# A selective-scan network: the first 512 tokens' chain written out in order, side work behind the chunk-end copies, eight scan buffers

## Chip, cores and metric

The kernel runs on one core of one Trainium2 chip. The metric is the device time of one execution in microseconds (us). Engines are named as in the profile: PE (TensorE), with its weight loads as PEld, DVE (VectorE), ACT (ScalarE), POOL (GpSimd) and SP (SyncE, which here issues all data transfers).

## What is computed

Two layers on an input of 4 images of 64 x 64 tokens with 128 channels, all in float32. The change touches only the first block, a two-dimensional selective scan (L is 4096 tokens, DI is 256 channels, N is 16 states, K is 4 directions):

```python
xz = layernorm(x) @ in_proj_w.T;  xh, z = split(xz);  z = silu(z)
xc = silu(depthwise_conv3x3(xh) + conv_b)                 # 256 channels, 64 x 64
xs = [xc by rows, xc by columns, both reversed]           # K = 4 orders of the tokens
dts, B, C = split(x_proj_weight @ xs)                     # 8 + 16 + 16 rows
delta = softplus(dt_projs_weight @ dts + bias);  A = -exp(A_logs)
for t in tokens:                                          # for each of 256 channels and 16 states
    h = exp(delta[t] * A) * h + (delta[t] * xs[t]) * B[t]
    y[t] = sum over states of h * C[t]
y = layernorm(sum of the 4 directions + D * xs) * z;  x = x + y @ out_proj_w.T
```

After it come a mixture of experts with token choice, a block of row, column and token projections, and a spectral convolution.

## The kernel before

**The scan.** The 4 batches, 4 directions and 8 pieces of 512 tokens make 128 chunks; each chunk has 16 steps, one for each state. A step works on two halves of 128 channels. ACT makes `da` (the exponential of delta times A, L2026) three steps ahead; SP loads `bc` (B and C of that state, spread over all partitions, L2016) five steps ahead into 6 buffers; DVE makes `db = du * B` in PSUM (L2078) and then runs the recurrence into `hh` (L2084); POOL saves the last column (`hst`, L2096) and multiplies `hh` by C (L2097); PE adds the result into `y` by eight transposing matmuls (L2124). `hh` has HH = 7 buffers, so DVE's scan of a step waits for the transposes of the step seven earlier. These waits are taken one step early, by a dependency set by hand.

**A chunk's sizes.** `step_sizes` (L1894) prepares delta (`dl`) and `dx = delta * xc` of the next chunk while the present one runs, one piece a step: load `dts` and `xc`, project (`dt_ps`), softplus on ACT with a correction on POOL, sum on PE (`dl_ps`), product on POOL. At the last step of a chunk `into_psum` (L2003) copies `dx` with ACT into the two PSUM tiles `du` that DVE reads; they have one buffer, so the copies wait for the last db of the chunk, and the first db of the next chunk waits for them.

**Side work.** Everything else of the first part (normalising, input projection, convolution, row projections and gating of the other batches, experts) is a Python generator that yields an estimated cost with each piece. `deal` (L1960) is called twice a step, pulls pieces until what was made reaches what is due, and hangs what it pulled behind the scan's latest instruction on each engine. What is due grows by `WEIGHT[batch] / (chunks * (16 - len(BUSY)) * 2)` a call; in the steps listed in BUSY nothing is dealt. Side work has two PSUM banks (`bank`, L274), and evictions are put off to the next piece (`evict_soon`). The recording layer then orders each engine's instructions itself, within the dependencies.

**The front.** The first batch can't hide behind a scan. `front` (L404) works in groups of 512 tokens (g = 0 to 7): sums for the norm on DVE (L429, L431), reciprocal root on ACT, refinement on POOL (L435 to L441), normalising on ACT, transposes on PE (L448), input projection (L454), copies into the padded image `xh` (L457), a 3 x 3 convolution, sigmoid on ACT (L398 to L401), gate on POOL (L482), row projections (L489), stores of dts, B and C (`put_bc_of`). For groups 0 and 1 the convolution's half 0 runs on DVE (nine taps, L478 and L480) and half 1 on PE (matmuls with diagonal matrices, L467); groups 2 and 3 are done together, both halves on DVE. All of groups 0 to 3 and the input of group 4 are issued ahead of the scan, as are the sizes of chunk 0 (`prelude`); groups 4 to 7 are dealt beside the scan. At the start of chunks 0 to 7 pieces are pulled until the rows of the next chunk's group have been issued. Then come the columns (the transposed image and its projections), batches 1 and 2, gates and filters.

Of the kernel before, what the change touches and what calls it, by code (L numbers as in the profile page):

```python
# [32 lines left out]

FIRST = 1
WEIGHT = (1180.0, 1008.0, 1346.0, 927.0)

BUSY = (2, 3)
XB = 6
HH = 7
AHEAD = 4  # L40
# [66 lines left out]
def kernel(  # L107
# [58 lines left out]
    early = tc.tile_pool(name="fr_x", bufs=XB, side="right")  # L166
# [7 lines left out]
    for g in range(5):  # L174
        load_x0(g)
# [7 lines left out]
    nc.sync.dma_start(cb, conv_b)  # L183
    xp = wp.tile([P, 2, 2, 104], F32, name="xp")
# [6 lines left out]
    nc.sync.dma_start(aneg, a_logs)  # L191
    dsk = wp.tile([P, K, 2], F32, name="dsk")
# [17 lines left out]
    for h in range(2):  # L210
        for t in range(9):
            nc.vector.tensor_scalar(diag[:, h, t, :], ident, cw[:, h, t : t + 1], None, ALU.mult)
# [191 lines left out]
    def front(prelude):  # L404
# [6 lines left out]
        with tc.tile_pool(name="fr", bufs=2) as fr:  # L411
            pools = ExitStack()
            fps = pools.enter_context(tc.tile_pool(name="fr_ps", bufs=2, space=PSUM))
            xps = pools.enter_context(tc.tile_pool(name="fr_xd", bufs=1, space=PSUM))
            xh = [fr.tile([P, H + 2, W + 2], F32, name=f"xh{h}", bufs=1) for h in range(2)]
            for h in range(2):
                nc.gpsimd.memset(xh[h][:, 0, :], 0.0)
                nc.gpsimd.memset(xh[h][:, H + 1, :], 0.0)
                nc.gpsimd.memset(xh[h][:, 1 : H + 1, 0:1], 0.0)
                nc.gpsimd.memset(xh[h][:, 1 : H + 1, W + 1 : W + 2], 0.0)  # L420
            st, xn, vs, sts = {}, {}, {}, {}

            def sums(g):
                s6 = fr.tile([P, 4, 6], F32, name="s6")
                mv = fr.tile([P, 4, 2], F32, name="mv", bufs=4)
                r = fr.tile([P, 4], F32, name="f_r", bufs=4)
                nm = fr.tile([P, 4], F32, name="f_m", bufs=4)
                for q in range(4):
                    nc.vector.bn_stats(s6[:, q, :], x0[g][:, q, :])  # L429
                for q in range(4):  # L430
                    nc.vector.bn_aggr(mv[:, q, :], s6[:, q, :])  # L431
                nc.scalar.activation(r, mv[:, :, 1], AF.Ln, bias=eps6)
                nc.scalar.activation(r, r, AF.Exp, scale=-0.5)
                a = fr.tile([P, 4], F32, name="f_a")
                nc.gpsimd.tensor_scalar(a, mv[:, :, 1], 1.0, 1e-6, ALU.mult, ALU.add)  # L435
                nc.gpsimd.tensor_mul(a, a, r)
                nc.gpsimd.tensor_mul(a, a, r)
                nc.gpsimd.tensor_scalar(a, a, -0.5, 1.5, ALU.mult, ALU.add)
                nc.gpsimd.tensor_mul(r, r, a)
                nc.gpsimd.tensor_scalar(nm, mv[:, :, 0], -1.0, 0.0, ALU.mult, ALU.add)  # L440
                nc.gpsimd.tensor_mul(nm, nm, r)  # L441
                st[g] = nm, None, r

            def spread(g):
                norm_apply(x0[g], x0[g], st[g], 4)
                ps = bank([P, 4, P], "xt_ps")
# [3 lines left out]
                nc.scalar.copy(xn[g], ps.rearrange("c q p -> c (q p)"))  # L450
                nc.sync.dma_start(xn_d[b][:, 512 * g : 512 * (g + 1)], xn[g])
                for h in range(2):
                    ps = bank([P, 8, W], "in_ps")
                    nc.tensor.matmul(  # L454
                        ps, w_in_t[:, h * P : (h + 1) * P], xn[g], start=True, stop=True
                    )
                    nc.scalar.copy(xh[h][:, 1 + 8 * g : 9 + 8 * g, 1 : W + 1], ps)  # L457

            def windows(h, t, r0, rows):
                dy, dx = divmod(t, 3)  # L460
                return xh[h][:, r0 + dy : r0 + dy + rows, dx : dx + W]

            def convolve(g0, n, h, first):
                ps = fps.tile([P, 8 * n, W], F32, name="fcv_ps", tag="cv")
                for g in range(n):
                    for t in range(first):
                        nc.tensor.matmul(  # L467
                            ps[:, 8 * g : 8 * g + 8],
                            diag[:, h, t, :],
                            windows(h, t, 8 * (g0 + g), 8),  # L470
                            start=(t == 0),
                            stop=(t == first - 1),
                        )
                for t in range(first, 9):
                    wt = cw[:, h, t : t + 1]
                    src = windows(h, t, 8 * g0, 8 * n)
# [4 lines left out]
                v, e = sigmoid_of(fr, ps.rearrange("p r w -> p (r w)"), h)  # L481
                nc.gpsimd.tensor_mul(v, v, e)  # L482
                nc.sync.dma_start(xc_d[b][0, h, :, 512 * g0 : 512 * (g0 + n)], v)
                for g in range(n):
                    vs[g0 + g, h] = v[:, 512 * g : 512 * (g + 1)]

            def project(g, ps):
                for h in range(2):
                    nc.tensor.matmul(ps, xp[:, 0, h, :], vs[g, h], start=(h == 0), stop=(h == 1))  # L489
                sts[g] = fr.tile([104, SC], F32, name="xd_st", bufs=3)  # L490
                evict_soon(lambda: nc.scalar.copy(sts[g], ps))

            def rows_of(g):
                project(g, xps.tile([104, SC], F32, name="fxd_ps"))
                put_bc_of(b, g, sts[g])

            for g in range(5):
                sums(g)
            for g in range(5):
                if g + 5 < 8:  # L500
                    load_x0(g + 5)
                    sums(g + 5)
                spread(g)
                if g in (1, 2):
                    for h in range(2):
                        convolve(g - 1, 1, h, 9 * h)
                if g == 2:
                    rows_of(0)
                    prelude(sts[0])
            for h in range(2):  # L510
                convolve(2, 2, h, 0)
            for g in range(1, 4):
                rows_of(g)
            side["rows"] = AHEAD
# [3 lines left out]
            for g in range(5, 8):  # L518
                norm_apply(x0[g], x0[g], st[g], 4)
                yield 1.5  # L520
                ps = bank([P, 4, P], "xt_ps")
                for q in range(4):
                    nc.tensor.transpose(ps[:, q, :], x0[g][:, q, :], ident)
                xn[g] = fr.tile([P, 512], F32, name="xn")
                evict_soon(lambda ps=ps, g=g: nc.scalar.copy(xn[g], ps.rearrange("c q p -> c (q p)")))
                yield 1.0
                settle()
                yield 0.5
                nc.sync.dma_start(xn_d[b][:, 512 * g : 512 * (g + 1)], xn[g])
                for h in range(2):  # L530
                    ps = bank([P, 8, W], "in_ps")
                    nc.tensor.matmul(
                        ps, w_in_t[:, h * P : (h + 1) * P], xn[g], start=True, stop=True
                    )
                    nc.scalar.copy(xh[h][:, 1 + 8 * g : 9 + 8 * g, 1 : W + 1], ps)
                    yield 1.0

            def rows(g):
                project(g, bank([104, SC], "xd_ps"))

            for g in range(AHEAD, 8):
                for h in range(2):
                    ps = bank([P, 8, W], "cv_ps")
                    for t in range(9):
                        nc.tensor.matmul(
                            ps,
                            diag[:, h, t, :],
                            windows(h, t, 8 * g, 8),
                            start=(t == 0),
                            stop=(t == 8),  # L550
                        )
                        if t % 3 == 2:
                            yield 2.6
                    v, e = sigmoid_of(fr, ps.rearrange("p r w -> p (r w)"), h)
# [16 lines left out]
                rows(g)  # L571
# [1311 lines left out]
    with ExitStack() as c0:  # L1883
        pb = c0.enter_context(tc.tile_pool(name="pb", bufs=2))
        slots(3)


# [6 lines left out]
        def step_sizes(b, k, ci, have=None):  # L1894
# [6 lines left out]
            def pieces():  # L1901
                cs = slice(ci * SC, (ci + 1) * SC)
                dts = have
                if dts is None:
                    dts = pb.tile([R, SC], F32, name="dts", bufs=1)
                    nc.sync.dma_start(dts, dts_d[b][k, :, cs])
# [79 lines left out]
        def prelude(st):  # L1986
            sizes[0] = step_sizes(0, 0, 0, st[0:R, :])
            list(sizes[0][3])

        opening = front(prelude)  # L1990
        next(opening)
        side.pop("pool").close()
        dbs = c0.enter_context(tc.tile_pool(name="pb_db", bufs=1, space=PSUM))
# [246 lines left out]
```

## Time and profile before

| what | us |
|---|---|
| median of 3 runs (lowest, highest) | 9501.18 (9497.8, 9502.11) |
| the profiled execution | 9507.07 |
| its span in the trace | 9505.2 |
| first db of the scan, from the span's start | 83.15 |
| last scan ends | about 7711 |
| busy in the span: DVE, PE, POOL, ACT | 8222.5, 7331.8, 6373.1, 6138.1 |
| mean of one scan (with a start value), one db, one da | 1.258, 0.677, 0.718 |
| mean of one POOL product of hh and C | 2.359 |

Times in the trace count from the span's start. A row of a timeline gives start, duration, engine, line, operation, output and inputs, shapes, how many were merged, and in brackets how long the engine was idle before and what ended that. A row of waits gives who waited for whom, the total, the number of times and the longest. On PE a float32 matmul of a 512-wide tile appears as two MATMUL rows, a transposing one as a single row. The program calls fcv_ps the convolution's PSUM tile, sg_e and sg_v the sigmoid's, fxd_ps the row projection's.

### The profile page before, as it was taken

What the parts mean: (1) busy time and instruction counts of PE and PEld (TensorE: products, weight loads), DVE (VectorE), ACT (ScalarE), POOL (GpSimd) and SP (SyncE); (2) the same over time, 40 slices, a digit from 0 to 9 for tenths busy, and PEclk for the clock granted to TensorE, in tenths of its full rate; (3) what the DMA queues carried; (4) which work ended last, traced back from release to release, by engine and by line L of the source; (5) the groups of instructions that cost most, each with busy time, mean ns of one, the idle gap of its engine ahead of it and who ended that gap; (6) DMA issues with size and microseconds to landing.
All of it is one profiled execution on the core that took longest, in us unless ns stands there. A gap on an engine that the chain in (4) does not pass through costs nothing.

```text
span 9505.2 us, 139568 instructions
## 1 busy us (share of the span) xinstructions
PE 7331.8 (77%) x45462; PEld 4748.2 (50%) x45462; DVE 8222.5 (87%) x9171; ACT 6138.1 (65%) x11727; POOL 6373.1 (67%) x5954
## 2 busy tenths in 40 slices
PE   7687886577677777697778777767777677999997
PEld 3444544355444555454545554544555445555553
DVE  8999999989999999999999999999999951566663
ACT  6676767657755676776855677765676744555552
POOL 6788888869788888887878788978888841000000
PEclk8788787678787877798878787878887876999998
DMA  5656566667566656658757667757656673333336
GB/s 161 228 189 218 191 213 223 206 189 243 174 221 224 207 163 207 192 192 256 230 183 244 195 195 233 242 172 239 226 164 207 211 220 95 91 95 95 95 94 181
DMA packets 914957, 1806.23 MB, mean 190 GB/s; under 512 B 86816, under 2 KB 472640, under 8 KB 910520
## 3 DMA queue, kind: packets, MB, share of 16 engines
q1 hardware_dynamic: 914232, 1797.30, 60.1%
q8 instruction: 365, 5.98, 0.3%
q14 instruction: 360, 2.95, 0.1%
HBM read 1554.75 MB, written 242.22 MB: 189 GB/s over the span
## 4 chain that ended last, share of the span: by engine, by line
POOL 23%; PE 20%; issue 11%; DVE 10%; ACT 7%; DMA 6%; SPq 0%; POOLq 0%; DVEq 0%; ACTq 0%
POOL hh L2097 17%; PE sp_ps L1674 10%; DVE hh L2084 4%; DVE wt L1678 3%; PE y L2124 3%; ACT da L2026 2%; DVE db L2078 2%; DMA bc<-bc_d 1%; POOL hst L2096 1%; PE dl_ps L1940 1%; POOL dx L1943 1%; POOL ex L1934 1%; ACT no_sq L352 1%; DMA yk<-y_d 1%; PE yk_ps L790 1%
## 5 line engine op out<-in xcount | busy, mean ns | idle before, releaser
L2097 POOL TENSOR_TENSOR hh<-hh,bc 128x1024 f32<-128x1024 f32 x2048 | 4830.2, 2359 | 365.8 <-DVE hh L2084 203.2
L2084 DVE TENSOR_TENSOR_SCAN hh<-da,hst,db 128x512 f32<-128x512 f32 x3584 | 4375.6, 1258 | 117.3 <-PE y L2124 54.3
L2124 PE MATMUL y<-ident,hh 128*128 128x128 f32 x16384 | 2654.6, 316 | 1233.2 <-POOL hh L2097 1125.3
L2026 ACT ACTIVATE da<-dl,aneg 128x512 f32<-128x512 f32 x4096 | 2776.0, 718 | 1135.4 <-DVE hh L2084 1124.5
L2124 PEld LDWEIGHTS y<-ident,hh 128*128 128x128 f32 x16384 | 2212.5, 163 | 2147.7 <-POOL hh L2097 1502.3
L2078 DVE TENSOR_TENSOR db<-du,bc 128x512 f32<-128x512 f32 x4096 | 2605.0, 677 | 149.6 <-ACT du L2007 128.3
L2096 POOL COPY hst<-hh 128x2 f32<-128x2 f32 x1792 | 336.6, 188 | 695.6 <-DVE hh L2084 629.1
L1678 DVE COPY wt<-sp_ps 128x1024 f32<-128x1024 f32 x512 | 606.0, 1220 | 176.3 <-PE sp_ps L1674 153.2
L1674 PE MATMUL sp_ps<-vt,taps 32*128 32x256 f32 x8192 | 588.7, 399 | 54.7 <-DVE wt L1678 35.1
L2084 DVE TENSOR_TENSOR_SCAN hh<-da,db 128x512 f32<-128x512 f32 x512 | 594.5, 1199 | 12.3 <-PE y L2124 9.7
L1678 ACT COPY wt<-sp_ps 128x1024 f32<-128x1024 f32 x512 | 516.5, 1015 | 102.3 <-PE sp_ps L1674 82.4
L1674 PEld LDWEIGHTS sp_ps<-vt,taps 32*128 32x128 f32 x8192 | 387.9, 184 | 246.9 <-DVE wt L1678 196.8
L1678 DVE COPY zs<-sp_ps 128x1024 f32<-128x1024 f32 x128 | 156.7, 1224 | 353.1 <-PE sp_ps L1674 350.9
L1674 PE MATMUL sp_ps<-wt,ut 128*32 128x256 f32 x8192 | 448.7, 379 | 1.4 <-DVE wt L1678 1.4
L661 PE MATMUL cv_ps<-xh,diag 128*128 128x512 f32 x864 | 402.1, 601 | 2.8 <-ACT sg_v L399 2.5
L1915 PE MATMUL dt_ps<-dts,dtw 8*128 8x512 f32 x508 | 352.3, 794 | 47.0 <-ACT sg_v L399 21.5
L1940 PE MATMUL dl_ps<-ex,ident 128*128 128x512 f32 x512 | 307.0, 688 | 95.2 <-POOL ex L1934 95.1
L1674 PEld LDWEIGHTS sp_ps<-wt,ut 128*32 128x32 f32 x8192 | 264.8, 110 | 193.8 <-issue 23.5
L1943 POOL TENSOR_TENSOR dx<-dl,xc 128x1024 f32<-128x1024 f32 x128 | 302.5, 2363 | 84.0 <-ACT dl L1941 76.0
L1941 ACT COPY dl<-dl_ps 128x512 f32<-128x512 f32 x256 | 148.0, 578 | 306.4 <-PE dl_ps L1940 305.8
L1934 POOL TENSOR_TENSOR ex<-ex,dx 128x1024 f32<-128x1024 f32 x128 | 302.3, 2362 | 59.3 <-ACT dx L1931 52.0
L1678 ACT COPY zs<-sp_ps 128x1024 f32<-128x1024 f32 x128 | 129.5, 1012 | 320.7 <-DMA zf<-zs 168.8
(331 smaller groups left out, 9260.0 us busy)
## 6 DMA issues: line engine op xcount, KB each, us to landing
bc<-bc_d SPq DMA_DIRECT2D x2048, 512.0 KB
xc<-xc_d SPq DMA_DIRECT2D x128, 512.0 KB
y_d<-ys SPq DMA_DIRECT2D x128, 512.0 KB
w1t<-in_w_dram SPq DMA_DIRECT2D x96, 512.0 KB
w2t<-in_w_dram SPq DMA_DIRECT2D x192, 256.0 KB
yk<-y_d SPq DMA_DIRECT2D x128, 256.0 KB
yk<-y_d SPq DMA_DIRECT2D x256, 128.0 KB
zf<-zs SPq DMA_DIRECT2D x512, 64.0 KB
```

Source lines behind the costliest of these rows:

```text
L661: nc.tensor.matmul(ps, diag[:, h, t, :], xh[:, 8 * g + dy : 8 * g + dy + 8, dx : dx + W], start=(t == 0), stop=(t == 8),)
L1674: tc.keep_in_program_order(nc.tensor.matmul(*args, **kw))
L1678: tc.keep_in_program_order(copy(dst, src))
L1934: nc.gpsimd.tensor_sub(ex, ex, dx)
L1940: nc.tensor.matmul(ps, ident, t[:, h], start=t is dl, stop=t is w)
L1943: nc.gpsimd.tensor_mul(dx, dl, xc)
L2026: i_act = nc.scalar.activation(das[t][:, h, :], sizes[t // N][0][:, h, :], AF.Exp, scale=aneg[:, tk, h, t % N : t % N + 1],)
L2078: nc.vector.tensor_mul(db[h], dus[i][h], bcs[s][:, 0, :])
L2084: i_dve = nc.vector.tensor_tensor_scan(o, d0, d1, init, ALU.mult, ALU.add)
L2096: nc.gpsimd.tensor_copy(hsts[t // N][:, :, t % N], hhs[t][:, :, last])
L2097: i_pool = nc.gpsimd.tensor_mul(hhs[t], hhs[t], bcs.pop(t)[:, 1:2, :].to_broadcast([P, 2, SC]))
L2124: i_pe = nc.tensor.matmul(ys[c][:, q, h, :], hhs[t][:, h, q * P : (q + 1) * P], ident, is_transpose=True, start=(n == 0 and k > 0 and q % ...
```

## The change

1. The front is rewritten along the chain of group 0, its order on PE, ACT, DVE and POOL fixed as it is written. Normalising is split over DVE and ACT, refinement of groups 0 to 2 is on DVE; the diagonal matrices are built by POOL (18 products) instead of DVE; the gates of group 0 are one DVE operation each. Ahead of the scan now stand group 0, the input of groups 1 and 2, the taps of group 1 (half 0 on DVE, half 1 on PE), and the sums of all groups. Chunk 0's sizes are made by `first_sizes`, half by half, with DVE's product written straight into `du`. The weights needed first are loaded ahead of x0's later groups.
2. The rest of groups 1 to 7 is dealt beside the scan, all taps on PE; `WEIGHT[0]` rises from 1180 to 1275. ACT work that is pulled at the start of chunks 0 to 7 is ordered behind the exponentials that were issued two steps before.
3. Step 14 joins BUSY, and after the copies of `into_psum` the anchor for dealt ACT work is the second copy.
4. HH rises from 7 to 8. x0 gets 8 buffers instead of 6, and the pools for `du` and `db` change places.

The core of the diff:

```diff
-WEIGHT = (1180.0, 1008.0, 1346.0, 927.0)
-BUSY = (2, 3)
-XB = 6
-HH = 7
-AHEAD = 4
+WEIGHT = (1275.0, 1008.0, 1346.0, 927.0)
+BUSY = (2, 3, 14)
+HH = 8
...
-    for g in range(5):
+    for g in range(2):
         load_x0(g)
...
+    load_x0(2)
...
+    for g in range(3, 8):
+        load_x0(g)
...
-    for h in range(2):
-        for t in range(9):
-            nc.vector.tensor_scalar(diag[:, h, t, :], ident, cw[:, h, t : t + 1], None, ALU.mult)
...
+            for h in (1, 0):
+                for t in range(9):
+                    nc.gpsimd.tensor_scalar(
+                        diag[:, h, t, :], ident, cw[:, h, t : t + 1], None, ALU.mult
+                    )
...
+            def refine(g):
+                nm, _, r = st[g]
+                a = fr.tile([P, 4], F32, name="f_a")
+                var = mv[g][:, :, 1]
+                nc.vector.scalar_tensor_tensor(a, var, 1e-6, r, ALU.add, ALU.mult)
+                nc.vector.tensor_mul(a, a, r)
+                nc.vector.tensor_scalar(a, a, -0.5, 1.5, ALU.mult, ALU.add)
+                nc.vector.tensor_mul(r, r, a)
+                nc.vector.scalar_tensor_tensor(nm, mv[g][:, :, 0], -1.0, r, ALU.mult, ALU.mult)
...
+            def apply(g):
+                nm, _, r = st[g]
+                for q in range(4):
+                    x, rq, mq = x0[g][:, q, :], r[:, q : q + 1], nm[:, q : q + 1]
+                    if q % 2:
+                        nc.vector.tensor_scalar(x, x, rq, mq, ALU.mult, ALU.add)
+                    else:
+                        nc.scalar.activation(x, x, AF.Identity, bias=mq, scale=rq)
...
+            moments(0)
+            scales(0)
+            moments(1)
+            refine(0)
+            scales(1)
+            apply(0)
+            refine(1)
+            apply(1)
+            keeps = [turned(g, own([P, 4, P], "xt_ps")) for g in range(2)]
+            moments(2)
+            scales(2)
+            moments(3)
+            for keep in keeps:
+                keep()
+            moments(4)
+            refine(2)
+            apply(2)
+            for g in range(2):
                 for h in range(2):
+                    widen(g, h, own([P, 8, W], "in_ps"))()
+            cv = [[t.rearrange("p (r w) -> p r w", w=W) for t in banks_of_du()]]
+            taps_dve(cv[0][0], 0, 0, range(9))
+            taps_pe(cv[0][1], 0, 1, range(6))
+            keep = turned(2, own([P, 4, P], "xt_ps"))
+            keep()
+            taps_pe(cv[0][1], 0, 1, range(6, 9))
+            e0 = sigmoid(cv[0][0], 0)
+            cv.append([bank([P, 8, W], "cv_ps") for _ in range(2)])
+            taps_dve(cv[1][0], 1, 0, range(3))
+            places = [widen(2, h, own([P, 8, W], "in_ps")) for h in range(2)]
+            gated(0, 0, cv[0][0], e0)
+            e1 = sigmoid(cv[0][1], 1)
+            for place in places:
+                place()
+            taps_dve(cv[1][0], 1, 0, range(3, 5))
+            gated(0, 1, cv[0][1], e1)
+            xd = own([104, SC], "fxd_ps")
+            rows_of(0, 0, xd)
+            taps_pe(cv[1][1], 1, 1, range(2))
+            rows_of(0, 1, xd)
+            rows_done(0, xd)
+            put_bc_of(b, 0, sts[0])
+            taps_dve(cv[1][0], 1, 0, range(5, 9))
+            moments(5)
+            chain = first_sizes(sts[0], own)
+            next(chain)
+            taps_pe(cv[1][1], 1, 1, range(2, 9))
+            moments(6)
+            next(chain)
+            moments(7)
+            next(chain, None)
+            last = {}
+            for ins in traced[begin:]:
+                if ins.engine in PINNED:
+                    if ins.engine in last:
+                        tc.add_manual_dep(ins, last[ins.engine], order, reason="as written")
+                    last[ins.engine] = ins.name
+            side["rows"] = 1
...
+        def first_sizes(st, own):
...
+            for h in range(2):
+                steps.append(own([P, SC], "dt_ps"))
+                nc.tensor.matmul(
+                    steps[h], dtw[:, 0, h * P : (h + 1) * P], st[0:R, :], start=True, stop=True
+                )
+            for h in range(2):
+                bias = dtb[:, 0, h : h + 1]
+                nc.scalar.activation(ex[:, h], steps[h], AF.Abs, bias=bias)
+                nc.scalar.activation(ex[:, h], ex[:, h], AF.Exp, scale=-1.0)
+            yield
+            for h in range(2):
+                bias = dtb[:, 0, h : h + 1]
+                nc.scalar.activation(dl[:, h], steps[h], AF.Relu, bias=bias)
+                nc.vector.tensor_scalar(w[:, h], ex[:, h], 1.0, None, ALU.add)
+                nc.vector.tensor_scalar(dx[:, h], w[:, h], -1.0, None, ALU.add)
+                nc.vector.tensor_sub(ex[:, h], ex[:, h], dx[:, h])
+            for h in range(2):
+                nc.scalar.activation(w[:, h], w[:, h], AF.Ln)
+            yield
+            for h in range(2):
+                ps = own([P, SC], "dl_ps")
+                for t in (dl, ex, w):
+                    nc.tensor.matmul(ps, ident, t[:, h], start=t is dl, stop=t is w)
+                nc.scalar.copy(dl[:, h], ps)
+                nc.vector.tensor_mul(dus[0][h], ps, xc[:, h])
...
-            dus[i] = [bps.tile([P, SC], F32, name=f"du{h}") for h in range(2)]
+            dus[i] = banks_of_du()
             for h in range(2):
-                nc.scalar.copy(dus[i][h], sizes[i][1][:, h, :])
+                i_copy = nc.scalar.copy(dus[i][h], sizes[i][1][:, h, :])
+            return i_copy
...
-                    if i == 0:
-                        into_psum(0)
+                begin = len(traced)
                 if i < NSC and n == 0:
...
+                for ins in traced[begin:]:
+                    if ins.engine == mybir.EngineType.Activation:
+                        tc.add_manual_dep(ins, acts[s + 1], order, reason="queued behind")
...
                 if n == N - 1 and i + 1 < len(chunks):
-                    into_psum(i + 1)
+                    i_act = into_psum(i + 1)
```

`moments` are the sums of a group, `scales` the reciprocal root on ACT, `turned` the transposes, `widen` the input projection with its copy into `xh`, `taps_pe` and `taps_dve` the convolution's taps on either engine, `rows_of` and `rows_done` the row projection and its eviction. The pieces for groups 1 to 7 use the same helpers, with the refinement on POOL and the normalising on ACT.

## The prediction

> **What bounds the kernel now.** I read the engines' busy shares first, then the same table over four stretches, then VectorE's waits in the longest stretch, then the instructions around typical waits.
>
> ```profile
> PE 7331.8 (77%) x45462; PEld 4748.2 (50%) x45462; DVE 8222.5 (87%) x9171; ACT 6138.1 (65%) x11727; POOL 6373.1 (67%) x5954
> ```
>
> By stretch (length, then busy us of PE, PEld, DVE, ACT, POOL, then PEclk, DMA, GB/s):
>
> ```profile
> 0.00:83.15 83.15, 47.48 (x103) 19.67 (x104) 48.65 (x126) 52.18 (x100) 24.60 (x77) 0.88 0.40 128
> ...
> 560.70:2014.60 1453.90, 1090.74 (x4506) 676.32 (x4504) 1374.81 (x1564) 1000.52 (x1752) 1201.88 (x927) 0.80 0.63 204
> 2014.60:7711.00 5696.40, 4272.54 (x20501) 2849.21 (x20502) 5510.14 (x6229) 3879.60 (x8012) 4702.27 (x4409) 0.81 0.66 210
> 7711.00:9505.20 1794.20, 1563.11 (x18803) 977.50 (x18802) 835.41 (x743) 871.20 (x1220) 66.73 (x226) 0.92 0.41 116
> ```
>
> Three stages: a front of 83.15 us in which no engine is full; the scan, 7628 us, in which DVE is 95 to 97% busy; an end of 1794 us that the change doesn't touch. In the scan one undisturbed step (two db, two scans) starts 3.54 us after the one before; a chunk of 16 steps takes 56.6 us (54.7 for the first of a direction). There are 128 chunks, so only DVE's idle time, some 280 us, and the front can be won. The idle time, by what ended it (total, times, longest):
>
> ```profile
> DVE db L2078 <- ACT du L2007: 128.3, 50, 13.5
> DVE hh L2084 <- PE y L2124: 64.1, 35, 5.9
> DVE hh L2084 <- ACT da L2026: 20.4, 15, 3.6
> DVE db L2078 <- DMA bc<-bc_d: 18.1, 10, 7.2
> ```
>
> **Front: DVE begins at about 46 instead of 83.** The end of the old front on ACT:
>
> ```profile
> 74.33 1.11 ACT L398 ACTIVATE sg_e<-fcv_ps,ncb 128x1024 f32<-128x1024 f32 x1 [6.30 <-DVE fcv_ps L480]
> ...
> 82.52 0.60 ACT L2007 COPY du<-dx 128x512 f32<-128x512 f32 x1
> ```
>
> and on DVE:
>
> ```profile
> 63.43 16.05 DVE L480 SCALAR_TENSOR_TENSOR fcv_ps<-xh,cw,fcv_ps 128x1024 f32<-128x1024 f32 x13
> 83.15 0.70 DVE L2078 TENSOR_TENSOR db<-du,bc 128x512 f32<-128x512 f32 x1 [3.68 <-ACT du L2007]
> ```
>
> Everything the first chunk needs but the du copy is there by 68 us (exponentials from 58.5); the copy stands behind the sigmoids of groups 2 and 3, which wait for 18 DVE taps of 1.29 us (23 us). The change moves exactly these to PE beside the scan. The new chain, each duration from the row of the same instruction: x0 and its sums as now, to 6.0; refinement on DVE instead of POOL and half of the normalising, about 2.4 for two groups, 8.4; sums of group 2, 9.6. ACT then evicts two transposes, to 11.1. It next stands at the normalising of group 2, which waits for DVE's sums of 3 and 4 and its refinement (14.5); behind it wait the xh copies, and all taps behind these: first xh at 16.1, last at 17.7. Nine DVE taps of 0.78, to 23.2; on PE meanwhile nine taps at 0.88 (two passes of 0.44) and a transpose, 25.8. Two sigmoids (three ACT operations of about 0.65 each) and gates, 29; projection behind two taps, 30.6; eviction 31.2; dt 2.0, 33.2. Then PE holds seven taps of group 1 (6.2, to 39.4) ahead of the sums into dl_ps (2.8 each half: 42.2 and 45.0), while ACT and DVE finish softplus before 38. The du product and the first db follow at 45.8. Stores of the rows start at 31.3; now the first bc load is issued 4.2 us after its first row store (45.4 to 49.7), so bc is in by about 39: hidden, and late only if more than 6 us slower. Inside these times lie the sign flip of aneg on DVE, which waits for ACT's exponential at 11.3 (sums of 3 and 4 are queued behind it, hence 14.5), and the loads: SP issues one in 0.55 us, so x0 of groups 3 and 4, now eleventh and twelfth, are issued by 8 and land by 10 or 11, before 11.5; cw and cb come earlier than now. Moving the pools for db and du, and x0's two more buffers, cost nothing: no instruction comes with them. Saving 83.15 − 45.8 = 37 us; I allow 30 to 43, since the clock is unknown (four projection passes took 3.78 us cold, 1.88 later).
>
> One rule speaks against building the 18 diagonals on POOL beside DVE's refinement:
>
> ```profile
> 9.19 0.19 POOL L440 TENSOR_SCALAR f_m<-mv 128x4 f32<-128x4 f32 x1 [0.84 <-DVE mv L431]
> ...
> 11.71 0.31 POOL L435 TENSOR_SCALAR f_a<-mv 128x4 f32<-128x4 f32 x1
> ```
>
> The first is alone, the second runs while DVE builds the same diagonals (10.0 to 13.7): 0.12 us more. The Trainium skill, "SBUF — State Buffer", section "Who interferes with whom", says that a DVE copy or tensor_scalar in a two-port mode and a POOL instruction exclude each other for the whole instruction. The nearest POOL row of that shape takes 0.29 us (the 128x128 select); by the rule some 14 DVE operations could each lose that, 4 us; by the row 14 × 0.12 = 1.7 us. I put 1 us inside the 2.4 above, 4 in the range. The POOL diagonals themselves (18 × 0.29 = 5.3, from 6) are done at 11.5, five before PE needs them.
>
> **Groups 1 to 7 beside the scan.** Per group PE gets 18 taps (15.8 us); moved from DVE are 36 taps, 32 us of PE, with some 10 of projections and transposes; ACT's sigmoids move, and POOL's gates. Dealt units rise from 1180/32 = 36.9 to 1275/32 = 39.8 a chunk; a group costs 35. Before, chunks 0 to 3 took 55 to 57.9 us with 36.9 units of the same kind, so PE has room; I charge nothing there. New waits: each of chunks 0 to 6 puts six stores and the next chunk's dts load ahead of the bc loads on SP; the stores wait for the row eviction, dts for the stores' landing (some 4 us from first store). Behind them are bc loads five steps ahead, of which about 11 us is slack; a similar hold by the column store (10 us) cost 7.2 us once in chunk 4. Zero to 7 each; I take 5 in all. Columns come a chunk and a half later, with losses like today's (chunks 4 and 6: 10 and 14 us). The dense stage is the filters, chunks 28 to 32: 352 us against 5 × 56.6 = 283, PE late throughout. At 8% more units a chunk it spans 4.6 chunks; if its own work sets its time, 0.4 × 56.6 = 21 us of scan no longer fit into it. Between 0 and 21 I take 12. Together +17.
>
> **Side work behind the du copies; step 14 free.** The copies wait for the chunk's last db, and need 1.1 us. A loss:
>
> ```profile
> 501.67 1.67 ACT L373 ACTIVATE xt<-xt,no_m,no_r 128x128 f32<-128x128 f32 x4
> 503.22 1.34 ACT L2026 ACTIVATE da<-dl,aneg 128x512 f32<-128x512 f32 x2
> 504.44 1.11 ACT L2007 COPY du<-dx 128x512 f32<-128x512 f32 x2
> ```
>
> DVE then waited 4.38 us. In the orders of the two built programs, side instructions on ACT between the exponentials of next-chunk step 1 and the first copy fall from 450 to 271 over 127 boundaries; between step 0 and the copy only from 673 to 605. So much is merely moved one step earlier, where 3.54 − 1.34 = 2.2 us a step are free. Boundary by boundary: before chunks 7, 16, 30, 57 to 60, 78 and 118 to 119 the block ahead of the copy is gone or small; before 122 to 127 (2.2 us each) it is as it was, before 27, 31 and 102 longer. I take 128 to 83: −45, between 0 and −100. The wait has a follower: evictions queued behind a copy hold one of the two side PSUM banks, PE waits for the bank, and y behind it.
>
> **An eighth hh buffer.** Matched by step, nearly all the waits put down to y are PE's: POOL had finished the awaited step 15 to 20 us before, PE 0.2 us before. So an extra buffer is one step (3.54 us) of slack, less what the six bc buffers limit, which they don't while POOL is on time.
>
> ```profile
> 4433.60 2.45 DVE L2084 TENSOR_TENSOR_SCAN hh<-da,hst,db 128x512 f32<-128x512 f32 x2 [5.86 <-PE y L2124]
> ```
>
> This one falls to 2.3; isolated waits below 3.5 go; the run at 1934 to 2037 keeps most. Of 64.1 I take −40, between −15 and −55.
>
> **Sum.** −37 − 45 − 40 + 17 = −105. The profiled execution took 9507.07 us (span 9505.2 and 1.9 around it), 5.9 over the median 9501.2; it becomes 9402, the median 9396.
>
> **Rivals.** (a) *The waits only change their name*: DVE, no longer held at copies, runs into late PE (77% busy) and ACT; of 85 us some 25 stays won: −37 − 25 + 17 = −45, 9456. For it: side work is the same, and 8% denser in batch 0; against it: PE and ACT idle a quarter to a third of the scan. (b) *The copies go free*: du waits to 30, y to 10: −37 − 98 − 54 + 5 = −184, 9317. For it: clean boundaries show copies 0.1 us after db; against it: the unchanged order at a third of the lossy boundaries. (c) *Slower*: group rows late in chunks 0 to 6. SP's stores block bc, and the next chunk's dt, softplus and du start late; price: lateness beyond the 11 us of slack, seven times. With the gains of (a) it must exceed (45 + 20)/7 = 9 us a chunk, 20 us late at each row eviction; 15 us over would give 9456 + 105 = 9561. For it: one 10 us hold cost 7.2; against it: in the new order the rows stand at the end of a chunk, fourteen steps before du is needed. (d) *The edit misses*, du waits hold: 9396 + 40 = 9436.
>
> **Numbers.** Forecast (9355 to 9425) 0.52; (a) and (d), 9425 to 9482, 0.29; (b) 0.11; within 0.2% (19 us, about what a measurement of this kernel can tell from no change) 0.04; (c) 0.04. The range 9345 to 9458 takes the forecast, most of (a) and (d), and the edge of (b). Faster 0.92, same 0.04, slower 0.04.
>
> **What would show it.** First db at 42 to 50 us; chunk 8 begins 450 to 485 us later; du waits near 83; y waits near 24; chunks 28 to 32 no shorter. I am wrong if du waits stay above 110, if y or bc waits grow, or if the front ends after 55.

## The result, and the profile after

The changed kernel takes 9476.9 us (median of 10 runs, 9461.7 to 9486.1), the kernel before 9501.7 in the same comparison: a ratio of 0.9971, with a 95% interval of 0.9962 to 0.9981. It is faster by 25 us, where 105 were forecast (range 9345 to 9458). The profiled execution took 9481.75 us, its span 9480.0.

The stretches of the changed kernel, cut at its first db, at chunk 8, at the end of batch 0's scan and at the last scan (columns as in the prediction):

```profile
0.00:49.00 49.00, 36.02 (x81) 15.39 (x81) 33.28 (x122) 23.65 (x46) 12.14 (x32) 0.97 0.54 171
49.00:540.20 491.20, 370.90 (x1593) 230.29 (x1594) 453.88 (x512) 324.44 (x569) 384.94 (x322) 0.85 0.58 198
540.20:2023.10 1482.90, 1133.48 (x4614) 699.22 (x4614) 1376.90 (x1563) 1040.07 (x1885) 1208.54 (x963) 0.80 0.62 203
2023.10:7687.00 5663.90, 4263.63 (x20440) 2831.11 (x20439) 5508.46 (x6228) 3876.16 (x8005) 4705.80 (x4409) 0.81 0.65 210
```

The front is 34 us shorter. But batch 0's scan, the second and third line, takes 1974.1 us, against 1931.4 before: its end comes 8.5 us later than before, so the front's gain is gone there. The fourth line, batches 1 to 3, is 32 us shorter than before (5696). VectorE's waits within the scan:

```profile
DVE db L2181 <- ACT du L2107: 115.6, 68, 7.7
DVE hh L2187 <- PE y L2227: 66.9, 34, 7.4
DVE db L2181 <- DMA bc<-bc_d: 31.9, 17, 6.8
DVE hh L2187 <- ACT da L2127: 18.2, 15, 3.2
```

Against the lines of before, du fell by 13 where 45 were forecast, y rose by 3 where 40 less were forecast, and bc grew by 14. All of DVE's waits in the scan together, the smaller ones included, were 285 us before and are 291 now. By parts of the profiled executions, in us from the start of a batch's first chunk to that of the next:

| | before | changed | front_only |
|---|---|---|---|
| first db | 83.2 | 49.0 | 49.2 |
| batch 0 | 1931.4 | 1974.1 | 1950.4 |
| batch 1 | 1878.8 | 1850.3 | 1875.1 |
| batch 2 | 1919.9 | 1927.6 | 1919.9 |
| batch 3 | 1897.5 | 1886.0 | 1896.9 |
| after the last scan | 1794.5 | 1793.0 | 1794.6 |

The last column is the first experiment: the new front with its side work, without the three small edits.

### The profile page after: what moved, and what is told of

It is laid out like the page before. It is cut to its first block, busy times and chain, and to the rows that moved or that the text cites. A ratio compares the mean times of both kernels' runs of the same rounds, so it can differ in the third digit from the quotient of the medians.

```text
span 9480.0 us, 139641 instructions
## 1 busy us (share of the span) xinstructions
PE 7363.5 (78%) x45534; PEld 4751.1 (50%) x45534; DVE 8208.7 (87%) x9166; ACT 6137.1 (65%) x11725; POOL 6378.8 (67%) x5949
## 4 chain that ended last, share of the span: by engine, by line
POOL 34%; PE 25%; issue 14%; DVE 10%; ACT 8%; DMA 8%; SPq 1%; POOLq 0%; DVEq 0%; ACTq 0%
POOL hh L2200 25%; PE sp_ps L1744 10%; DVE hh L2187 4%; PE y L2227 4%; DVE wt L1748 3%; PE dl_ps L2047 3%; ACT da L2127 2%; DMA bc<-bc_d 2%; DVE db L2181 2%; POOL hst L2199 2%; POOL dx L2050 1%; POOL ex L2041 1%; PE cv_ps L731 1%; ACT no_sq L356 1%; PE dt_ps L2022 1%
```

## The experiments

I call the three small edits **A** (the anchor of ACT's side work behind the second du copy), **S** (step 14 closed to dealing) and **H** (the eighth hh buffer). All ratios are to the kernel before, timed beside each run (medians 9497.8 to 9506.1, so the ratio is the thing to compare). Differences in the text are of medians; where the ratios give another number that matters, it stands beside. Waits are those of the profiled execution. The other runs follow in the text.

| run | what it is | median us | ratio (95%) | du | y | bc | da |
|---|---|---|---|---|---|---|---|
| before | | 9501.7 | 1 | 128 | 64 | 18 | 20 |
| changed | front + A + S + H | 9476.9 | 0.9971 (0.9962–0.9981) | 116 | 67 | 32 | 18 |
| front_only | front | 9486.0 | 0.9981 (0.9974–0.9987) | 124 | 83 | 19 | 16 |
| edits_only | A + S, old front | 9488.3 | 0.9986 (0.9979–0.9992) | 82 | 98 | 32 | 25 |
| density_only | old front, WEIGHT[0] 1275 | 9536.7 | 1.0040 (1.0027–1.0054) | 139 | 99 | 24 | 19 |
| anchor_alone | front + A | 9471.7 | 0.9969 (0.9956–0.9981) | 117 | 79 | 20 | 15 |
| seven_hh | front + A + S | 9491.4 | 0.9990 (0.9982–0.9998) | 90 | 109 | 19 | 16 |
| step14_dealt | front + A + H | 9470.3 | 0.9970 (0.9960–0.9981) | 127 | 47 | 39 | 33 |
| anchor_before | front + S + H | 9494.3 | 0.9997 (0.9989–1.0005) | 133 | 60 | 34 | 28 |
| seven_bc | changed, seven bc buffers | 9499.9 | 0.9998 (0.9990–1.0007) | 125 | 102 | 11 | 36 |
| eight_hh_order_of_seven | front + A + H, order of anchor_alone | 9423.7 | 0.9916 (0.9902–0.9929) | 128 | 13 | 53 | 15 |
| changed_order_of_seven | changed, order of seven_hh | 9432.0 | 0.9928 (0.9915–0.9942) | 109 | 27 | 53 | 25 |

**Front and small edits apart.** front_only undoes A, S and H in the changed kernel; edits_only puts A and S, without H, into the kernel before; density_only only raises its dealing.

```diff
 # front_only
-BUSY = (2, 3, 14)
-HH = 8
+BUSY = (2, 3)
+HH = 7
...
-                    i_act = into_psum(i + 1)
+                    into_psum(i + 1)
 # density_only, in the kernel before
-WEIGHT = (1180.0, 1008.0, 1346.0, 927.0)
+WEIGHT = (1275.0, 1008.0, 1346.0, 927.0)
```

> The changed kernel with three edits undone: seven hh buffers, step 14 dealt again, side work on ACT anchored as before (not behind the second du copy). What is left of the change is the new front and groups 1 to 7 beside the scan. Theory A (the waits of the scan only change their name; the three edits are worth little): 9470 to 9495, within 15 us of the changed kernel; du waits 110 to 135, y 55 to 80. Theory B (each edit earned what the prediction gave it, and the denser first batch spent it): 9540 to 9565, du waits about 160, y about 105.

> The kernel before with only step 14 added to the idle steps and the side work on ACT anchored behind the second du copy. Theory A: 0 to 20 us faster than before, du waits 110 to 125, some of it lost to y and bc. Theory B: 40 to 50 us faster, du waits about 83, y and bc as before.

> The kernel before with WEIGHT[0] raised from 1180 to 1275: the same side work in batch 0, dealt 8 per cent denser. Theory C (the density costs batch 0 its gain): chunk 32 begins 15 to 30 us later than before (2030 to 2045), most of it in the filters' last chunks. Theory D (the denser dealing is free, and what was lost in batch 0 is the chain of the groups' rows in chunks 0 to 8): chunk 32 begins within 6 us of before, time within 8 us of before.

front_only lost 19.0 us in batch 0, after it won 34 in front; the prediction had +17 for this. Its total lies where theory A put it (y, at 83, just outside). density_only was 46 us slower in batch 0 (1977.5), beyond what theory C expected, and at another place. Its filters now run in chunks 26 to 29 and cost about what they did (73 us over undisturbed chunks, 69 in chunks 28 to 32 before); most of the rest was lost in chunks 0 to 25 (1565 us against 1528). An open step is one in which side work is dealt; the units are those of its estimated cost. front_only deals the same 1275/(32 x 14) = 2.85 units per open step and lost 19, so the density alone doesn't set the price: which pieces are dealt, and beside what, counts too. The waits of edits_only within the scan:

```profile
DVE hh L2085 <- PE y L2125: 97.6, 38, 6.9
DVE db L2079 <- ACT du L2007: 82.2, 40, 5.7
```

The du waits are at 82, just as predicted for the changed kernel. But y rose by 33 and bc by 13, and the time fell by 13 only, as theory A had it. One bc wait reads as a du wait under a new name. The first db of chunk 30, amid the filters, in the kernel before:

```profile
1875.63 0.70 DVE L2078 TENSOR_TENSOR db<-du,bc 128x512 f32<-128x512 f32 x1 [13.47 <-ACT du L2007]
```

and in edits_only:

```profile
1867.99 1.30 DVE L2079 TENSOR_TENSOR db<-du,bc 128x512 f32<-128x512 f32 x2 [15.25 <-DMA bc<-bc_d]
```

Chunk 29, which ends with this wait, takes 73.3 us in the one and 71.9 in the other. Of the 33 us that y rose, most stands in batch 2, which is dealt most densely (3.10 units per open step before, 3.34 with S): chunks 69, 70, 73, 78 and 93 gained 22 us of y waits, and batch 2 became 11 us longer while batch 1 (2.32, then 2.50 units) became 15 shorter.

**The eighth buffer, step 14 and the anchor, each undone.** seven_hh sets HH to 7 in the changed kernel, step14_dealt sets BUSY to (2, 3), anchor_before drops the `i_act =`; anchor_alone undoes H and S together.

> The changed kernel with seven hh buffers. Theory A (the order of PE stands one part of a step closer to the scan when there is one buffer more, and the late episodes hang on chains tied to the scan itself): within 10 us of the changed kernel, y waits 60 to 80. Theory B (the buffer earned its 40 us but other edits added as many y waits): 30 to 40 us slower than the changed kernel, y waits 100 to 110.

> The changed kernel with step 14 dealt again (BUSY of two steps); eight buffers and the anchor behind the copy stay. Theory E (what decides is the side work dealt per open step: batch 0 has 1275/(32 x 13) = 3.06 units a step with step 14 closed and 2.85 with it open, batch 2 3.34 and 3.10; above about 2.9 units PE falls behind): against the changed kernel batch 0's scan (1974) is 15 to 30 us shorter, batch 2 (1928) 5 to 10 shorter, batch 1 (1850) 10 to 25 longer, batch 3 (1886) 0 to 10 longer; in all 0 to 15 us faster. Theory G (closing step 14 costs nothing, the anchor behind the copy does): batch 0 stays within 8 us of 1974, in all 10 to 25 us slower, the du waits being larger in every batch.

> The changed kernel with the side work on ACT anchored as before, not behind the second du copy; eight buffers and a closed step 14 stay. Theory E: with step 14 closed little is left that the anchor moves; within 10 us of the changed kernel, batch 0 stays above 1960. Theory G: batch 0 15 us shorter or more, the other batches as long or longer.

> The changed kernel with seven hh buffers and step 14 dealt: the new front and the anchor behind the second du copy alone. If the three edits simply added up (front 9486, all three 9477), about 9475 to 9480, du waits about 105. Theory E (each edit takes its own waits away, and the queue of side work returns them as others): du waits fall by 10 to 25 against the front alone (124), y (83) and bc (19) rise by nearly as much, 9476 to 9490; the eighth buffer then is worth more after the anchor than before it.

seven_hh's waits within the scan:

```profile
DVE hh L2187 <- PE y L2227: 109.0, 44, 8.3
DVE db L2181 <- ACT du L2107: 90.3, 46, 7.0
```

So neither theory was whole: the buffer does take 42 us of y away (109 to 67), as B said, and yet the time falls by 14 us only (18 by the ratios), for du rises by 25 and bc by 12. Step 14 behaves as theory E said: reopened, batch 0 is 19 us shorter, batch 2 6.5 shorter, batch 1 15 and batch 3 8.5 longer, every one in the stated window. Closing it trades du for y: 117 to 90 against 79 to 109 with seven buffers, and 20 us are lost (9471.7 to 9491.4). Of anchor_before neither theory was right: without A the time is 17 us worse (25 by the ratios; du 116 to 133), so A is worth something with step 14 closed too. The parts don't add: front and A alone are as fast as all (9471.7 and 9476.9, overlapping intervals).

**One more bc buffer.** If each wait were a loss of its own, the bc waits would be next.

```diff
-    early = tc.tile_pool(name="fr_x", bufs=8, side="right")
+    early = tc.tile_pool(name="fr_x", bufs=6, side="right")
...
-            t = s + 5
+            t = s + 6
...
-                bcs[t] = pb.tile([P, 2, SC], F32, name="bc", bufs=6)
+                bcs[t] = pb.tile([P, 2, SC], F32, name="bc", bufs=7)
```

> The changed kernel with seven bc buffers instead of six, loaded six steps ahead instead of five (x0 gets six buffers, so that it fits). If waits are losses of their own, the 32 us of bc waits fall below 8 and the kernel is 20 us faster or more. Theory A (the wait shows only where DVE meets a late queue): bc waits fall below 10, the du and y waits rise by most of it, time within 10 us of the changed kernel.

bc fell by 20 us, y rose by 35, and the kernel is 23 us slower than the changed one. Theory A had the direction of the waits, but not that the time could grow this much.

**The filters.** Chunks 28 to 31 take 302 us in the changed kernel, 75 over undisturbed ones; there batch 0 deals `filters`, which mixes four candidate filters by scalings on ACT and additions on POOL. filters_later deals the same pieces in batch 1 instead, with the weights moved; filters_later_b2_open opens step 14 in batch 2 besides.

```diff
-WEIGHT = (1275.0, 1008.0, 1346.0, 927.0)
+WEIGHT = (1142.0, 1141.0, 1346.0, 927.0)
...
-            yield from filters()
...
+        if b == 1:
+            yield from filters()
```

> The changed kernel with the filters (133 of batch 0's 1275 units) dealt first in batch 1: WEIGHT is 1142, 1141, 1346, 927, so per open step 2.75 units in batch 0 and 2.83 in batch 1 (2.50 in the changed kernel). Theory E: batch 0 25 to 45 us shorter than 1974, batch 1 5 to 25 longer than 1850, in all 10 to 30 us faster than the changed kernel. Theory A (what is won at one place is lost at another, whatever the density): within 8 us of the changed kernel.

> As the run before, and step 14 is dealt in batch 2 alone (3.10 units a step there instead of 3.34). Theory E: batch 2 5 to 12 us shorter than 1928, the rest as in the run before; 15 to 40 us faster than the changed kernel. Theory A: within 8 us of the changed kernel.

Both missed: 9498.2 (0.9990 to 1.0007) and 9493.2 (0.9987 to 1.0004), slower than the changed kernel. Batch 0 fell by 56 us to 1918, in spite of a single bc wait of 33 us in chunk 7 (91 us long), where the columns, now dealt more thinly, were not done in time: from 513 to 534 us SP issues their stores one behind another, ahead of the bc loads. But batch 1 rose by 76. In it, chunks 33 to 37 were 68 us over undisturbed ones at 2.83 units a step: the filters cost about the same at a lower density, as they did at 2.85 units in density_only, so theory E's 2.9 units are no threshold for them. What they wait for is seen on POOL, here in the kernel before:

```profile
1850.67 2.49 POOL L988 TENSOR_TENSOR accm<-accm,mt 128x512 f32<-128x512 f32 x2
1853.12 0.18 POOL L2096 COPY hst<-hh 128x2 f32<-128x2 f32 x1
1853.37 2.35 POOL L2097 TENSOR_TENSOR hh<-hh,bc 128x1024 f32<-128x1024 f32 x1
```

and in the window around it (PE, PEld, DVE, ACT, POOL as before):

```profile
1850.00:1900.00 50.00, 29.99 (x125) 22.07 (x124) 33.63 (x38) 32.49 (x67) 48.96 (x41) 0.57 0.65 212
```

POOL's scan work in a step is 2.35 + 0.18 of 3.54 us, so less than one addition fits, and often two are dealt. POOL is busy 49 of 50 us, DVE only 34. The prediction read PE as "late throughout"; PE was, but because its y products stood waiting for POOL (1840 to 1900):

```profile
PE y L2124 <- POOL hh L2097: 25.3, 9, 5.2
```

And the du wait of 13.47 us shown above leads back to POOL in part: ACT, which made that copy only at 1875.02, had before it stood 5.31 us for a POOL addition of the filters:

```profile
1866.98 0.69 ACT L998 ACTIVATE me<-me,sg 128x128 f32<-128x128 f32 x2 [5.31 <-POOL me L994]
```

filters_on_pe sums on PE. It also takes the scalings off ACT and loads a block ahead:

```diff
-                            nc.scalar.activation(mt[:, 0:m], mt[:, 0:m], AF.Identity, scale=h)
-                            nc.gpsimd.tensor_add(acc[:, ks], acc[:, ks], mt[:, 0:m])
...
+                    nc.tensor.matmul(
+                        ps[:, 0:m], hd[:, i, :], mts[i][:, 0:m], start=(i == 0), stop=(i == 3)
+                    )
```

> The changed kernel with the sums over the four candidate filters made by PE (matmuls with hard[i] times the identity, summed in PSUM, loads one block ahead) instead of ACT scalings (0.72 each) and POOL additions (1.27 each); same dealt cost. Theory P (chunks 28 to 31 are slow because POOL is full: 2.36 + 0.2 of a step's 3.54 are the scan's own, and two additions a step don't fit): chunks 28 to 32 take 240 to 260 us instead of 302, in all 30 to 55 us faster than the changed kernel. Theory Q (they are slow by PE, as my prediction said, or by the density): 290 us or more there, the same time in all or slower.

> As the run before, and step 14 is dealt in batches 0 and 2, where the dealing is dense, and closed in 1 and 3. Theory E: batch 0 10 to 20 us and batch 2 5 to 10 us shorter than in the run before, 10 to 25 us faster than it. Theory A: within 8 us of it.

9453.1 (0.9934 to 0.9959), and 9440.3 with step 14 open in batches 0 and 2 (0.9925 to 0.9952). Chunks 28 to 31 fell to 271, 29 and 30 to 57.7 and 56.4 each, and in a window around the one above DVE is full again (POOL, still 57 of 60 us busy, now just keeps up):

```profile
1840.00:1900.00 60.00, 39.13 (x176) 28.17 (x174) 58.99 (x68) 45.81 (x92) 57.21 (x44) 0.76 0.64 209
```

Theory P has the direction, and about half of the size it gave to these chunks (its 302 us is the time of chunks 28 to 31); the 24 us in all lie below its 30 to 55, and the last chunk of the stage still takes 87 us. The run alone doesn't part POOL from ACT and the loads, which it relieves too; that POOL was the full engine is read from the window before (49 of 50 us, ACT 32). Opening step 14 gave 6 us in batch 0 and 9 in batch 2; the 13 us between the medians lie within overlapping intervals.

**Time for a late load.** On the latter kernel, ten empty units were put between the loads of a batch's first row projections and the first projection on PE.

> The kernel of filters_on_pe_open (9440) with two empty pieces of 5 units between the loads of a batch's first row projections and the first of these on PE (10 units a batch, WEIGHT[0] 1295 and WEIGHT[2] 1356). Theory R (much of the y waits is PE standing in its order in front of a projection whose input is still on its way through copy, store and load; some 16 us at chunk 71): y waits fall from 54 to 30 or less, 10 to 25 us faster. Theory A (the queue returns it, and the density rises by 1.6 and 0.7 per cent): within 8 us of 9440.

9443.5 (0.9922 to 0.9949), y 53 as before: theory R fell. Giving that load time doesn't help; why, the run doesn't show.

**The order.** What returned the buffer's gain? The traces of seven_hh and of the changed kernel, which differ in the hh buffer alone, hold the same instructions in another order. Matched by name and counted against the scan's own steps, of 6347 side instructions on ACT 561 stand later, nearly all by one step, and 26 earlier; on POOL 142 and 7, on SP 168 and 6, on PE 30 and 2; on DVE some db and scans change places. So with one buffer more the recording layer puts some of ACT's, POOL's and SP's side work a step later. To take this away, the order of all five engines was read from the program built with seven buffers and imposed on the kernel with eight:

```diff
+    for text in ORDER.values():
+        places = np.cumsum(np.frombuffer(zlib.decompress(base64.b85decode(text)), "<i4"))
...
+            tc.add_manual_dep(ins, last.name, order, reason="pinned")
```

> The kernel of step14_dealt (new front, anchor behind the copy, step 14 dealt, eight hh buffers), with the order of the instructions on PE, ACT, DVE, POOL and SP fixed to the one of anchor_alone, which differs from it in the number of hh buffers alone. The recording layer itself moves 86 of 31417 PE instructions, 1171 of 10482 on ACT, 361 on POOL, 376 on SP by a few places when the buffer is added. Theory O (these moves spend the buffer's slack): y near 47, bc, da and du as in anchor_alone (20, 15, 118), so 25 to 35 us faster than anchor_alone (9472): 9437 to 9447. Theory A (the side work's queues at run time return the waits whatever the order): bc plus da 45 us or more, du 120 or more, within 10 us of 9470.

> The changed kernel itself (eight hh buffers, step 14 closed, anchor behind the copy), with the order of the instructions on PE, ACT, DVE, POOL and SP fixed to the one of seven_hh, which differs in the number of hh buffers alone. Theory O (the recorder's moves spend the buffer's slack): y waits fall from seven_hh's 109 to 20 to 50, du and bc stay near 90 and 20 or rise by a third of that; 9430 to 9450, which is 30 to 45 us faster than the changed kernel. Theory A: within 10 us of 9477.

9423.7 and 9432.0: 47 and 45 us faster than the same kernels in the layer's own order (51 and 41 by the ratios), 48 and 59 faster than with seven buffers in that order. In the traces of either pair of seven and eight buffers, all five engines run the same sequence of instructions (45534 on PE, 11725 on ACT, 9166 on DVE, 5949 on POOL, 5548 on SP), so of all that the traces count, nothing but the buffer differs there. The waits of changed_order_of_seven within the scan:

```profile
DVE db L2181 <- ACT du L2107: 109.0, 59, 7.8
DVE db L2181 <- DMA bc<-bc_d: 52.7, 18, 8.1
DVE hh L2187 <- PE y L2227: 26.5, 11, 5.0
```

y falls from seven_hh's 109 to 26.5. Theory O has the time in both pairs, and more than it expected in the first. It doesn't have all the waits: in the first pair bc and da together (67) and du (128) lie where theory A put them, and y fell to 13, not 47; in the second, some 40% of what y lost came back as bc (19 to 53). That the six bc buffers are the next limit, once POOL may lag a step more, fits this, but no run tried more of them with the order fixed.

Then filters and order together, and an order recorded for six buffers:

> Both together, to see whether they add: new front, anchor, step 14 dealt, filters summed by PE, eight hh buffers, and the order of the same program recorded with seven. If the filters (-24) and the order (-48) add up: 9395 to 9410. If the order had taken the same loss as the filters: 9415 to 9430.

> As the run before, with the order recorded for six hh buffers, run with eight. Theory O, if one more step kept free is worth more: y waits near zero, 5 to 15 us faster than the run before. If the order for six places side work so late that copies and the next chunk's sizes come late: du and da waits grow, the same or slower.

9421.6 (0.9901 to 0.9928) and 9421.5 (0.9903 to 0.9930). These are the fastest medians, but they can't be told from the order alone (9423.7). 9421.6 lies where the order would have taken the same loss as the filters, and 12 us from where the gains would add. Still, whether they add stays open: the profiled execution of filters_pe_order_of_seven was 25 us shorter than that of eight_hh_order_of_seven, the timed ones overlap (9407.7 to 9428.9, and 9417.8 to 9432.8). A step more of slack in the order did nothing more, as the second expectation had it: y went from 13 to 6, du from 102 to 124.

## Why the prediction was wrong, by its steps

- **Front, −37: right.** First db at 49.0, −34.2. Of the 3.2 us over 45.8, most are PE's seven taps of group 1, and DVE's du product, which waits for ACT's eviction of the same sums (a row of PE, a stretch with the columns of the tables above, a row of DVE):

```profile
33.92 7.97 PE L500 MATMUL cv_ps<-xh,diag 128*128 128x512 f32 x14
35.00:38.00 3.00, 3.00 (x5) 1.35 (x4) 2.87 (x7) 2.92 (x6) 0.00 (x0) 0.50 0.75 246
48.18 0.70 DVE L2001 TENSOR_TENSOR du<-dl_ps,xc 128x512 f32<-128x512 f32 x1 [2.36 <-ACT dl L2000]
```

  The taps take 7.8 us to the next start (41.73) where 6.2 were reckoned: from 35 to 38 us the granted clock is 0.50, while it is 1.00 before 34 and after 39. So the sums of the first half end, and those of the second begin, at 44.3 instead of 42.2. The prediction allowed for the clock in its range; its word "cold" for the 3.78 us of the old projection isn't shown, for the granted clock reads 1.00 in both stretches it compares.
- **POOL's diagonals beside DVE: the row was nearer than the rule.** They took about 0.6 us each, not 0.29, and ended at 16.6:

```profile
6.04 10.58 POOL L427 TENSOR_SCALAR diag<-ident,cw 128x128 f32<-128x128 f32 x18 [3.93 <-DMA cw<-in_conv_w_dram]
```

  Of the fifteen DVE operations on 128x4 of the refinement five took 0.10 to 0.19 us longer than their like, 0.7 in all: 1.7 was worked out from the row, 4 from the rule of the Trainium skill ("SBUF — State Buffer", "Who interferes with whom"). None was held for the 0.6 us of a whole POOL instruction. Whether any of them ran in a two-port mode, of which the rule speaks, the trace doesn't show.
- **Groups 1 to 7 and density, +17: right in sum, by luck.** front_only measured +19.0. But chunks 0 to 8 had 17 of it (1, 2, 7 and 8 grew, 4 shrank), where 5 were reckoned for the groups' rows and nothing more for the columns. The filters have 3 in chunks 28 to 31, and in 28 to 32, the prediction's stage, −5, where 12 were put. The named cause of the dense stage was wrong: it is POOL.
- **du, −45: the step failed in its last clause.** "2.2 us a step are free" priced the moved work on ACT alone. The du waits fell by 46 in edits_only, as reckoned, but S pushes the same units into 13 steps instead of 14, PE's included: y rose by 33, and 13 us were won where the removed waits count 46. In three pairs S costs 20, 7 and 8 us (seven buffers, eight, eight with the fixed order; the last two within overlapping intervals), and in the dense first batch it adds 14 us (1952 in anchor_alone, 1966 in seven_hh).
- **y, −40: the step failed in "an extra buffer is one step (3.54 us) of slack".** It is, if the order stays: 109 to 27, and 59 us. The recorded order does not stay; it spent the step on later side work, and 45 us were lost to that. In the layer's own order the buffer still took 42 us of y away, near the 40 forecast, but du and bc took 37 back: the wait was credited as time. The prediction compared the orders of the built programs for the copies and not for the buffer.
- **The sum.** From the profiles: −34.2 for the front, +19.0 for the denser batch 0, −4.3 in batches 1 to 3 between the kernel before and front_only, where no instruction of the scan was meant to move, −4.3 for A, S and H together where −85 was reckoned (−9 by the medians), −1.5 after the scan: −25. Rival (a) named what happened, waits that change their name, but kept 25 of the 85; even it was too hopeful. All three waits by which the prediction would know itself wrong in the scan came: du above 110 (116), y and bc grown (64 to 67, 18 to 32). A slip in its sums: rival (d), du waits that hold, adds 40 to 9396 where the du term is 45; that gives 9441.

Shown by runs: the trade of S with seven buffers, and the order's spending of H in two pairs. Shown by a window, and in part by a run: POOL as the limit of the filters. Not shown: what of front_only's 19 us is density and what the new pieces, why seven_bc lost 23 us (its order was not fixed, and x0 lost two buffers), and which move of the order costs most.

## What to carry to other kernels

A row of waits says where an engine meets a late one, not what is lost there: before crediting a removed wait, ask which queue was late and whether it is less late after the edit. When an order is made by a scheduling layer, an added buffer can change that order, so compare the built orders, or fix the order and add the buffer, before counting on its slack. Closing slots to side work makes the others denser; reckon units per open slot on every engine, POOL included.

## What was unexpected of the hardware

In the stretch where PE stands waiting for POOL, its granted clock falls and its y products get slower. The rows give the median between minimum and maximum, first at 1500 to 1560 us of the kernel before, then at 1840 to 1900, where the granted clock was 0.80 and 0.56:

```profile
L2124 PE MATMUL y<-ident,hh x152: 272/273/477, 1504.9 to 1559.3; 128*128 128x128 f32 x152
```

```profile
L2124 PE MATMUL y<-ident,hh x112: 272/421/477, 1841.0 to 1899.2; 128*128 128x128 f32 x112
```

PE was busy 43 of 60 us in the first and 34 in the second, so here the slower clock goes with less work, not more. It isn't the whole rule: in the front above the clock is 0.50 from 35 to 38 us with PE busy throughout, and its longest idle time in the ten us before that was 0.68 us. What sets the clock there, and whether slower y products lengthen the stall, no run shows. The other surprise is POOL's 0.6 us for a 128x128 product with a scalar per partition, twice the 0.29 of the select of that size.
